# Layer 3 of a four-layer graph network: half scores spread by GpSimd, carried by one product of ones, with a chunk's stages over three turns

## The chip, the cores and the metric

The kernel runs on one core of one Trainium2 chip. The metric is the device time of one execution in microseconds (us), the median of several executions. The core has four engines that matter here, each with its own in-order queue of instructions: TensorE (PE; its weight loads are listed apart as PEld), VectorE (DVE), ScalarE (ACT) and GpSimd (POOL). A fifth, SyncE (SP), issues DMA transfers. Engines wait for each other through semaphores.

## The reference, cut to what matters

The input x has 128 graphs of 64 nodes with 256 features each, and one 64x64 adjacency serves all graphs. Four layers run one after the other, each as x = x + layer(relu(layernorm(x))). Layer 0 is a graph convolution with LSTMs over windows, layer 1 an attention over 512 edges, layer 2 a graph convolution with two batch norms. The change is in layer 3, a dense attention:

```python
def _L3_gnn_ref(h, adj_matrix, W, a):
    Wh = jnp.einsum('bnf,fo->bno', h, W)
    a1, a2 = (a[:Fout, 0], a[Fout:, 0])
    s1 = Wh @ a1
    s2 = Wh @ a2
    e = s1[:, :, None] + s2[:, None, :]
    e = jnp.where(e >= 0, e, ALPHA * e)            # ALPHA = 0.2
    e = jnp.where(adj_matrix[None] == 0, -jnp.inf, e)
    attention = jax.nn.softmax(e, axis=-1)
    return jnp.einsum('bij,bjo->bio', attention, Wh)
...
h = jnp.maximum(_layernorm(x, axis=-1), 0.0)
x = x + _L3_gnn_ref(h, adj, L3_gnn_W, L3_gnn_a)
```

The score of a pair of nodes (i, j) is the sum of two half scores, s1 of the row node i and s2 of the column node j.

## The kernel before, in words

The 8192 tokens (graph times node) are cut into 16 chunks of 512. A chunk is four tiles of 128 partitions, and a tile holds two graphs of 64 nodes. All data is fp32. Layers 0, 1 and 2 run first over all chunks and end with a batch norm over all tokens, so layer 3 can't start a chunk before layer 2 has ended. Layer 3 then takes the chunks one by one. For chunk n its stages are:

- N(n), `second_norm` (L1884 and on): TensorE transposes the output of layer 2 (8 transposes, L1893); VectorE adds it to x (L1898) and takes the statistics of the layer norm (L1902, L1903); GpSimd turns them into scale and shift (L1912 to L1915) and normalizes four tiles (L1919). `scale_o` (L1881, GpSimd) prepares the input of the transposes.
- F(n), `features`: 8 transposes of the normalized tiles (L1934), and two ScalarE copies with relu into hT (L1937).
- W(n), `project3`: for each of the four tiles two products of hT with `wext`, which holds W and one more column, W a1 (L51, through the helper `mm`); ScalarE copies the 257 columns into `wh` (L1958). Column 256 of `wh` is s1.
- S(n), `dense_scores`: four products of hT with `wa2`, which holds the column W a2 repeated 64 times (L51). Their result is s2 of every column node, laid along the free axis and repeated on 64 partitions; the two graphs of a tile go to the two halves of the partitions. VectorE adds s1 (L1970), takes the leaky relu (L1976), adds the mask (L1977) and finds the negated row maximum (L1979). ScalarE takes four exponentials with their row sums (L1982), VectorE the reciprocal of the sums (L1985).
- X(n), `turn`: TensorE transposes the four tiles of exponentials (L1993); VectorE copies one half into a block-diagonal `field`, ScalarE the other half (L1997).
- V(n), `dense_values`: four products of `field` with `wh` (L51); VectorE scales them by the reciprocals and adds them to x (L2008); SP sends the chunk to memory (L2018, L2022).

The loop `for n in range(NCH + 1)` holds, in the order of the program: N(n+2), `scale_o`(n+4), F(n+1), the first two tiles of W(n), X(n-1), the other two tiles of W(n), S(n), V(n-1). The first turn differs: it ends W(0), then does S(0) and F(1).

A recording layer may move an instruction ahead of others on its engine. An instruction that is passed to `late` (which calls `tc.keep_in_program_order`) keeps its place. In layer 3 of the kernel before, `late` is used in the first three norms and in `scale_o` only. [...] PSUM is used as four single banks (`bank`) and two pairs of banks (`pair_bank`), each taken in turn; a tile of PSUM that is taken again waits for those who read it.

Of the kernel before, what the change touches and what calls it, by code (L numbers as in the profile page):

```python
# [17 lines left out]
P = 128  # L18
# [13 lines left out]
def gnn_stack_kernel(ctx: ExitStack, tc: tile.TileContext, a: dict, out: bass.AP):  # L32
# [17 lines left out]
    def mm(o, lhsT, rhs, start=True, stop=True):  # L50
        nc.tensor.matmul(o, lhsT, rhs, start=start, stop=stop)  # L51
# [145 lines left out]

    tab2 = ctx.enter_context(tc.tile_pool(name="tab2", bufs=1))
    bdH = tab2.tile([P, P], F32, tag="bdH", name="bdH")
    wext = tab2.tile([P, 2, D + 1], F32, tag="wext", name="wext")  # L200
    wa2 = tab2.tile([P, 2, T], F32, tag="wa2", name="wa2")
    mask3 = tab2.tile([P, T], F32, tag="mask3", name="mask3")

    def late_tables():
        with ExitStack() as setup:
            s2 = setup.enter_context(tc.tile_pool(name="s2", bufs=1, side="right"))
            nc.sync.dma_start(out=wext[:, :, :D], in_=a["W3"])
            w3T = s2.tile([P, 2, D], F32, tag="w3T", name="w3T")
            nc.sync.dma_start(out=w3T, in_=a["W3T"])
            a3 = s2.tile([P, 2, 2], F32, tag="a3", name="a3")  # L210
            nc.sync.dma_start(out=a3, in_=a["a3"])

            late(nc.vector.tensor_scalar(mask3, adj2, 0.0, NEG, ALU.is_equal, ALU.mult))
            yield

            eye = s2.tile([P, T], F32, tag="eye", name="eye")
            for h in range(2):
                r = slice(h * T, (h + 1) * T)
                nc.vector.tensor_copy(eye[r, :], ident[r, r])
            an = s2.tile([P, T], F32, tag="an", name="an")  # L220
            anT = s2.tile([P, T], F32, tag="anT", name="anT")
            nc.vector.tensor_tensor(an, adj2, eye, ALU.add)
            nc.vector.tensor_tensor(anT, adjT2, eye, ALU.add)
            yield
            deg = s2.tile([P, 3], F32, tag="deg", name="deg")
            diag = s2.tile([P, T], F32, tag="diag", name="diag")
            nc.vector.tensor_tensor(diag, an, eye, ALU.mult)
            nc.vector.tensor_reduce(deg[:, 0:1], anT, AX.X, ALU.add)
            nc.vector.tensor_reduce(deg[:, 1:2], an, AX.X, ALU.add)
            nc.vector.tensor_reduce(deg[:, 2:3], diag, AX.X, ALU.add)  # L230
            yield
            dinv = s2.tile([P, 1], F32, tag="dinv", name="dinv")
            nc.vector.tensor_tensor(dinv, deg[:, 0:1], deg[:, 1:2], ALU.add)
            nc.vector.tensor_tensor(dinv, dinv, deg[:, 2:3], ALU.subtract)
            nc.gpsimd.tensor_tensor(dinv, dinv, half_power[:, 0:1], ALU.pow)
            yield
            dinv_b = s2.tile([P, P], F32, tag="dinv_b", name="dinv_b")
            nc.vector.tensor_copy(dinv_b, dinv.to_broadcast([P, P]))
            nc.vector.memset(bdH, 0.0)
            nc.vector.tensor_scalar(anT, anT, dinv, None, ALU.mult)  # L240
            yield
            p = bank()
            mm(p[:, :T], dinv_b[:T, :], ident[:T, :T])
            yield
            for h in range(2):
                r = slice(h * T, (h + 1) * T)
                nc.vector.tensor_tensor(bdH[r, r], p[r, :T], anT[r, :], ALU.mult)
            yield

            p = bank()  # L250
            for c in range(2):
                for k in range(2):
                    mm(
                        p[:, 2 * c : 2 * c + 2],
                        w3T[:, k, c * P : (c + 1) * P],
                        a3[:, k, :],
                        k == 0,
                        k == 1,
                    )
            yield  # L260
            for c in range(2):
                nc.vector.tensor_copy(wext[:, c, D:], p[:, 2 * c : 2 * c + 1])
                nc.vector.tensor_copy(wa2[:, c, :], p[:, 2 * c + 1 : 2 * c + 2].to_broadcast([P, T]))
            yield


# [1212 lines left out]
    with ExitStack() as l2:  # L1479
# [463 lines left out]
        def project3(n, tiles):  # L1943

            if n not in att3:
                wh = t4.tile([P, 4, D + 1], F32, tag="wh", name="wh", bufs=3)
                att3[n] = [wh, None, None]
            for i in tiles:
                p = bank()
                for k in range(2):  # L1950
                    mm(
                        p[:, : D + 1],
                        hT3[n][:, k, i * P : (i + 1) * P],
                        wext[:, k, :],
                        k == 0,
                        k == 1,
                    )
                nc.scalar.copy(att3[n][0][:, i, :], p[:, : D + 1])  # L1958

        def dense_scores(n):  # L1960

            wh, hT = att3[n][0], hT3.pop(n)

            p = bank()
            for k in range(2):
                hv = hT[:, k, :].rearrange("p (i o t) -> p o i t", o=2, t=T)
                for h in range(2):
                    mm(p[h * T : (h + 1) * T, : 4 * T], wa2[:, k, :], hv[:, h], k == 0, k == 1)
            e = t4.tile([P, 4, T], F32, tag="e3", name="e3")
            nc.vector.tensor_tensor(  # L1970
                e,
                p[:, : 4 * T].rearrange("p (i t) -> p i t", t=T),
                wh[:, :, D:].to_broadcast([P, 4, T]),
                ALU.add,
            )
            nc.vector.scalar_tensor_tensor(e, e, 0.2, e, ALU.mult, ALU.max)  # L1976
            nc.vector.tensor_tensor(e, e, mask3.unsqueeze(1).to_broadcast([P, 4, T]), ALU.add)  # L1977
            nmx = stat.tile([P, 4], F32, tag="nmx3", name="nmx3")
            nc.vector.tensor_reduce(nmx, e, AX.X, ALU.max, negate=True)  # L1979
            den = stat.tile([P, 4], F32, tag="den3", name="den3")  # L1980
            for i in range(4):
                nc.scalar.activation(  # L1982
                    e[:, i, :], e[:, i, :], AF.Exp, bias=nmx[:, i : i + 1], accum_out=den[:, i : i + 1]
                )
            nc.vector.reciprocal(den, den)  # L1985
            att3[n][1:] = [e, den]

        def turn(n):

            e = att3[n][1]  # L1990
            p = bank()
            for i in range(4):
                nc.tensor.transpose(p[:T, i * P : (i + 1) * P], e[:, i, :], ident)  # L1993
            f = att3[n][1] = fields[n % 2]
            for h in range(2):
                r = slice(h * T, (h + 1) * T)
                (nc.scalar.copy if h else nc.vector.tensor_copy)(  # L1997
                    f[r, :, r], p[:T, :].rearrange("p (i j) -> p i j", i=4)[:, :, r]
                )

        def dense_values(n):
            wh, f, den = att3.pop(n)
            xt = xts.pop(n)
            p = pair_bank()
            for i in range(4):
                mm(p[:, i // 2, i % 2 * D : (i % 2 + 1) * D], f[:, i, :], wh[:, i, :D])
            for i in range(4):
                nc.vector.scalar_tensor_tensor(  # L2008
                    xt[:, i, :],
                    p[:, i // 2, i % 2 * D : (i % 2 + 1) * D],  # L2010
                    den[:, i : i + 1],
                    xt[:, i, :],
                    ALU.mult,
                    ALU.add,
                )
                if n == NCH - 1 and i % 2:

                    nc.sync.dma_start(  # L2018
                        out=token_tiles(out, n)[:, i - 1 : i + 1, :], in_=xt[:, i - 1 : i + 1, :]
                    )  # L2020
            if n < NCH - 1:
                nc.sync.dma_start(out=token_tiles(out, n), in_=xt)  # L2022
# [12 lines left out]
        for _ in second:  # L2035
            pass
        scale_o(3)
        for n in range(NCH + 1):
            if 4 <= n + 4 < NCH:
                fetch(n + 4)  # L2040
            if n + 2 < NCH:
# [1 line left out]
                    pass  # L2043
            if n + 4 < NCH:
                scale_o(n + 4)
            if n == 0:
                project3(0, (2, 3))
                dense_scores(0)
                features(1)
                continue  # L2050
            if n + 1 < NCH:
                features(n + 1)
            if 0 <= n < NCH:
                project3(n, (0, 1))
            if n >= 1:
                turn(n - 1)
            if 0 <= n < NCH:
                project3(n, (2, 3))
                dense_scores(n)
            if n >= 1:  # L2060
                dense_values(n - 1)

# [1 line left out]
def _laid_out(i):  # L2064
# [65 lines left out]
```

## Time and profile before

| what | us |
|---|---|
| median of 3 runs | 2017.27 |
| lowest and highest of these | 2010.04 and 2019.0 |
| time of the profiled execution | 2013.09 |
| span of its trace | 2011.2 |
| last product of layer 2 starts | 1851.2 |
| V(0) starts, V(11) starts | 1880.45, 1975.14 |
| V(12), V(13), V(14), V(15) start | 1983.74, 1992.21, 1999.07, 2004.02 |
| between V(n) and V(n+1), n from 0 to 11 | 8.60 to 8.61 |

From 1882 to 1984 us, 102 us, TensorE is busy 102.00, VectorE 79.72, ScalarE 51.24 and GpSimd 65.66, and the granted TensorE clock is 1.00 of full speed. Over the whole span TensorE is busy 1943.8 us (97%). An fp32 product appears as two MATMUL records, a transpose as one. In a timeline a line gives the start, the length, the engine, the source line and the operation, then what it writes and reads. The chain of waits follows the work that ended last back through time.

### The profile page before, as it was taken

To read this page: it belongs to the slowest core of one execution; us is meant where nothing else is said; L and a number is where in the kernel's file an instruction comes from. 1 tells how busy PE (TensorE), PEld (TensorE's weight loads), DVE (VectorE), ACT (ScalarE), POOL (GpSimd) and SP (SyncE) were. 2 spreads that over 40 slices of the span, in tenths; PEclk is the share of its full clock that TensorE was granted. 3 is DMA by queue.
4 is the path that set the end of the run, shared out by engine and by line. 5 is a ranking of instruction groups with operands and counts; after the bars stand their busy time and mean duration, and the time that the engine had idled before them with its cause. 6 is when DMAs were issued, how large, how long until landed. Compare 5 with 4: busy or idle time off the path is not lost. (4 is left out here: it accounts for less than half of the span.)

```text
span 2011.2 us, 25608 instructions
## 1 busy us (share of the span) xinstructions
PE 1943.8 (97%) x9464; PEld 1387.3 (69%) x9464; DVE 1309.0 (65%) x2468; ACT 1141.2 (57%) x2137; POOL 428.0 (21%) x590
## 2 busy tenths in 40 slices
PE   7999999999999999999999999999998999999998
PEld 6777478866678854888666888655555775444786
DVE  8764675575475567665655655657765877886776
ACT  4353775565455547665545555566664556691544
POOL 3000031030030011310200100336554510000563
PEclk9999999999999999999999999999999999999999
DMA  8422000010010053001001000612235641022012
GB/s 291 139 78 79 0 22 1 0 43 0 1 42 1 1 190 103 22 1 43 0 0 43 1 0 31 225 65 67 107 121 190 252 153 47 0 84 84 32 64 74
DMA packets 63869, 135.60 MB, mean 67 GB/s; under 512 B 6656, under 2 KB 41344, under 8 KB 61440
## 3 DMA queue, kind: packets, MB, share of 16 engines
q1 hardware_dynamic: 57504, 109.65, 16.3%
q0 software_dynamic: 5632, 24.12, 3.2%
q8 instruction: 74, 1.21, 0.3%
q14 instruction: 51, 0.42, 0.1%
q10 hardware_dynamic: 608, 0.20, 0.1%
HBM read 87.55 MB, written 46.40 MB: 67 GB/s over the span
## 5 line engine op out<-in xcount | busy, mean ns | idle before, releaser
L746 ACT ACTIVATE gate<-gate,bias 128x256 f32<-128x256 f32 (+2 forms) x368 | 247.2, 678 | 183.0 <-DVE gate L762 100.8
L718 PE MATMUL pa<-xop,sih 128*128 128x256 f32 (+2 forms) x1056 | 342.4, 417 | 8.3 <-DVE gate L772 8.1
L718 PEld LDWEIGHTS pa<-xop,sih 128*128 128x128 f32 x1056 | 198.8, 190 | 81.5 <-issue 21.5
L718 PE MATMUL pc<-xop,wih 128*128 128x256 f32 (+2 forms) x736 | 251.1, 423 | 0.0
L762 DVE TENSOR_TENSOR gate<-pb,gate 128x256 f32<-128x256 f32 (+2 forms) x184 | 87.4, 475 | 225.6 <-PE pb L718 151.3
L718 PE MATMUL pa<-lstm_h,shh 128*128 128x256 f32 (+1 forms) x672 | 212.7, 398 | 0.0
L718 PEld LDWEIGHTS pc<-xop,wih 128*128 128x128 f32 x736 | 139.8, 190 | 51.2 <-issue 23.0
L1086 ACT ACTIVATE lr<-pair 128x1024 f32<-128x1024 f32 x128 | 124.0, 1022 | 68.6 <-PE pair L1076 60.3
L777 DVE TENSOR_TENSOR gate<-pc,gate 128x256 f32<-128x256 f32 (+2 forms) x184 | 87.5, 475 | 112.3 <-PE pc L718 112.0
L718 PEld LDWEIGHTS pa<-lstm_h,shh 128*128 128x128 f32 x672 | 127.7, 190 | 30.2
L718 PE MATMUL pc<-lstm_h,whh 128*128 128x256 f32 (+1 forms) x448 | 141.8, 398 | 0.0
L1088 DVE SCALAR_TENSOR_TENSOR lr<-lr,fold 128x1024 f32<-128x1024 f32 x64 | 83.2, 1301 | 82.0 <-ACT lr L1086 79.4
L761 ACT COPY gate<-pa 128x256 f32<-128x256 f32 (+2 forms) x184 | 75.9, 413 | 93.0 <-PE pa L718 92.6
L1045 PE MATMUL bank<-wlv,hT 128*128 128x260 f32 x480 | 121.8, 397 | 0.5 <-issue 0.5
L772 DVE TENSOR_TENSOR gate<-pa,gate 128x256 f32<-128x256 f32 (+2 forms) x184 | 87.4, 475 | 43.7 <-PE pa L718 43.1
L746 ACT ACTIVATE gate<-pa,bias 128x256 f32<-128x256 f32 (+2 forms) x184 | 93.7, 509 | 30.9 <-PE pa L718 29.4
L1045 PEld LDWEIGHTS bank<-wlv,hT 128*128 128x128 f32 x480 | 86.8, 191 | 32.2 <-issue 11.2
L766 ACT COPY gate<-pa 128x256 f32<-128x256 f32 (+2 forms) x184 | 75.1, 408 | 53.1 <-PE pa L718 52.3
L718 PE MATMUL pa<-xop,wih 128*128 128x256 f32 (+1 forms) x320 | 101.6, 399 | 2.8 <-ACT xop L699 2.7
L718 PE MATMUL pb<-xop,wih 128*128 128x256 f32 (+1 forms) x320 | 100.4, 398 | 0.0
L718 PEld LDWEIGHTS pc<-lstm_h,whh 128*128 128x128 f32 x448 | 85.1, 190 | 20.1
L500 POOL TENSOR_TENSOR shh<-whh 128x512 f32<-128x512 f32 x6 | 8.3, 1389 | 385.5 <-DMA whh<-in_WhhT 317.6
(370 smaller groups left out, 3918.6 us busy)
## 6 DMA issues: line engine op xcount, KB each, us to landing
field<-keep SPq DMA_DIRECT2D x4, 2304.0 KB
wih<-in_WihT SPq DMA_DIRECT2D x8, 1024.0 KB, 7.1
xres<-in_x SPq DMA_DIRECT2D x16, 512.0 KB, 6.2
xa<-xres POOLq DMA_DIRECT2D x16, 512.0 KB
dense<-field POOLq DMA_DIRECT2D x4, 2048.0 KB
xin<-xb SPq DMA_DIRECT2D x16, 512.0 KB, 5.2
h<-xb SPq DMA_DIRECT2D x16, 512.0 KB, 3.7
xin<-in_x SPq DMA_DIRECT2D x15, 512.0 KB, 9.9
```

What stands on the lines that cost most here:

```text
L500: keep(nc.gpsimd.tensor_tensor(o, x, y, op))
L718: ins = nc.tensor.matmul(p[:, : self.N], weights[kind, self.phase](k, q), x[k], start=first_ and kind == "ih", stop=kind == "hh" or not se ...
L746: nc.scalar.activation(out, in_, AF.Tanh if q == 2 else AF.Sigmoid, bias=bias[:, self.w - 1, 2 * q + j : 2 * q + j + 1],)
L761: nc.scalar.copy(blk[0, 0], pa[:, :N])
L762: nc.vector.tensor_tensor(blk[0, 0], pb[:, :N], blk[0, 0], ALU.add)
L766: nc.scalar.copy(blk[1, 0], pa[:, :N])
L772: nc.vector.tensor_tensor(blk[1, 1], pa[:, :N], blk[1, 1], ALU.add)
L777: nc.vector.tensor_tensor(blk[1, 0], pc[:, :N], blk[1, 0], ALU.add)
L1045: ins = nc.tensor.matmul(o, hTs[n][:, k, i * P : (i + 1) * P], wlv[:, k, cols], start=k == 0, stop=k == 1)
L1086: nc.scalar.activation(lr, p, AF.Relu)
L1088: nc.vector.scalar_tensor_tensor(lrs[1], lrs[0], fold, lrs[1], ALU.mult, ALU.add)
```

## The change

The half score s2 no longer comes from products of its own. `wext` gets one more column, W a2, so `wh` has 258 columns and column 257 of it is s2 of the node on that partition. A new stage `spread` has GpSimd multiply this column with an identity pattern `eye`: `across[p, i, t]` is s2 of node p where t is the node's number in its graph, and zero elsewhere. One product with `same_graph`, a block-diagonal matrix of ones, adds `across` over the 64 partitions of a graph, which gives s2 of column node t on all partitions of that graph. VectorE then goes on as before.

The loop has one more turn, and its order is new: N(n+2), `scale_o`(n+4), V(n-2), S(n-1), F(n+1), W(n) with all tiles, `spread`(n), X(n-1). So the stages W and `spread`, then S and X, then V of a chunk stand in three successive turns, where before they stood in two. S's product, the first transpose of X and the first product of V are passed to `late`.

```diff
-    wext = tab2.tile([P, 2, D + 1], F32, tag="wext", name="wext")
-    wa2 = tab2.tile([P, 2, T], F32, tag="wa2", name="wa2")
+    wext = tab2.tile([P, 2, D + 2], F32, tag="wext", name="wext")
+    same_graph = tab2.tile([P, P], F32, tag="same_graph", name="same_graph")
+    eye = tab2.tile([P, T], F32, tag="eye", name="eye")
...
+            nc.vector.memset(same_graph, 0.0)
             for h in range(2):
                 r = slice(h * T, (h + 1) * T)
                 nc.vector.tensor_copy(eye[r, :], ident[r, r])
+                nc.vector.memset(same_graph[r, r], 1.0)
...
             for c in range(2):
-                nc.vector.tensor_copy(wext[:, c, D:], p[:, 2 * c : 2 * c + 1])
-                nc.vector.tensor_copy(wa2[:, c, :], p[:, 2 * c + 1 : 2 * c + 2].to_broadcast([P, T]))
+                nc.vector.tensor_copy(wext[:, c, D:], p[:, 2 * c : 2 * c + 2])
...
+        def spread(n):
+
+            wh = att3[n][0]
+            hT3.pop(n)
+            across = spreads[n] = t4.tile([P, 4, T], F32, tag="across", name="across")
+            nc.gpsimd.tensor_tensor(
+                across,
+                wh[:, :, D + 1 :].to_broadcast([P, 4, T]),
+                eye.unsqueeze(1).to_broadcast([P, 4, T]),
+                ALU.mult,
+            )
 
         def dense_scores(n):
 
-            wh, hT = att3[n][0], hT3.pop(n)
-
+            wh, across = att3[n][0], spreads.pop(n)
             p = bank()
-            for k in range(2):
-                hv = hT[:, k, :].rearrange("p (i o t) -> p o i t", o=2, t=T)
-                for h in range(2):
-                    mm(p[h * T : (h + 1) * T, : 4 * T], wa2[:, k, :], hv[:, h], k == 0, k == 1)
+            late(nc.tensor.matmul(p[:, : 4 * T], same_graph, across.rearrange("p i t -> p (i t)"), start=True, stop=True))
...
-        for n in range(NCH + 1):
+        for n in range(NCH + 2):
...
-            if n == 0:
-                project3(0, (2, 3))
-                dense_scores(0)
-                features(1)
-                continue
+            if n >= 2:
+                dense_values(n - 2)
+            if 1 <= n <= NCH:
+                dense_scores(n - 1)
             if n + 1 < NCH:
                 features(n + 1)
-            if 0 <= n < NCH:
-                project3(n, (0, 1))
-            if n >= 1:
+            if n < NCH:
+                project3(n, (0, 1, 2, 3) if n else (2, 3))
+                spread(n)
+            if 1 <= n <= NCH:
                 turn(n - 1)
-            if 0 <= n < NCH:
-                project3(n, (2, 3))
-                dense_scores(n)
-            if n >= 1:
-                dense_values(n - 1)
```

More of the change, by code (lines that the diff above doesn't have):

```diff
@@ L214, in late_tables @@
             yield
-            eye = s2.tile([P, T], F32, tag="eye", name="eye")
+            nc.vector.memset(same_graph, 0.0)
             for h in range(2):
@@ L1945, in project3 @@
             if n not in att3:
-                wh = t4.tile([P, 4, D + 1], F32, tag="wh", name="wh", bufs=3)
+                wh = t4.tile([P, 4, D + 2], F32, tag="wh", name="wh", bufs=3)
                 att3[n] = [wh, None, None]
@@ L1951, in project3 @@
                     mm(
-                        p[:, : D + 1],
+                        p[:, : D + 2],
                         hT3[n][:, k, i * P : (i + 1) * P],
@@ L1957, in project3 @@
                     )
-                nc.scalar.copy(att3[n][0][:, i, :], p[:, : D + 1])
+                nc.scalar.copy(att3[n][0][:, i, :], p[:, : D + 2])
+        spreads = {}
+        def spread(n):
[8 more added lines that the diff above has]
+            )
         def dense_scores(n):
-            wh, hT = att3[n][0], hT3.pop(n)
+            wh, across = att3[n][0], spreads.pop(n)
             p = bank()
-            for k in range(2):
-                hv = hT[:, k, :].rearrange("p (i o t) -> p o i t", o=2, t=T)
-                for h in range(2):
-                    mm(p[h * T : (h + 1) * T, : 4 * T], wa2[:, k, :], hv[:, h], k == 0, k == 1)
+            late(nc.tensor.matmul(p[:, : 4 * T], same_graph, across.rearrange("p i t -> p (i t)"), start=True, stop=True))
             e = t4.tile([P, 4, T], F32, tag="e3", name="e3")
@@ L1972, in dense_scores @@
                 p[:, : 4 * T].rearrange("p (i t) -> p i t", t=T),
-                wh[:, :, D:].to_broadcast([P, 4, T]),
+                wh[:, :, D : D + 1].to_broadcast([P, 4, T]),
                 ALU.add,
@@ L1992, in turn @@
             for i in range(4):
-                nc.tensor.transpose(p[:T, i * P : (i + 1) * P], e[:, i, :], ident)
+                ins = nc.tensor.transpose(p[:T, i * P : (i + 1) * P], e[:, i, :], ident)
+                if not i:
+                    late(ins)
             f = att3[n][1] = fields[n % 2]
@@ L2005, in dense_values @@
             for i in range(4):
-                mm(p[:, i // 2, i % 2 * D : (i % 2 + 1) * D], f[:, i, :], wh[:, i, :D])
+                ins = nc.tensor.matmul(
+                    p[:, i // 2, i % 2 * D : (i % 2 + 1) * D], f[:, i, :], wh[:, i, :D], start=True, stop=True
+                )
+                if not i:
+                    late(ins)
             for i in range(4):
```

## The prediction

> **What bounds the kernel now.** I read the page's first part, then the chain of waits in layer 3 alone, since the change touches nothing else that takes time. The page says that TensorE fills the span:
>
> ```profile
> PE 1943.8 (97%) x9464; PEld 1387.3 (69%) x9464; DVE 1309.0 (65%) x2468; ACT 1141.2 (57%) x2137; POOL 428.0 (21%) x590
> ```
>
> The chain of waits over one turn of layer 3 (start, us, what) holds TensorE and nothing else:
>
> ```profile
> 1938.02 2.75 PE bank L51 x16
> 1940.78 1.93 PE pair L51 x8
> 1942.70 0.87 PE pair L1893 x8
> 1943.58 1.30 PE bank L51 x6
> 1944.88 0.87 PE pair L1934 x8
> 1945.76 0.44 PE bank L51 x2
> 1946.19 0.44 PE bank L1993 x4
> ```
>
> The turn is V 1.93, N 0.87, six and two records of W, F 0.87, X 0.44, then eight of W and the eight of S (2.75). A W record takes 1.30/6 = 0.217, so W is 16 x 0.217 = 3.48 and S is 2.75 - 1.74 = 1.01. Sum 8.60, and the V starts are 8.60 to 8.61 apart: TensorE alone sets the pace. The others wait; over the 12 turns from 1882 to 1984 us the list of waits has
>
> ```profile
> ACT e L1982 <- DVE nmx L1979: 32.8, 12, 2.9
> DVE e L1970 <- PE bank L51: 20.2, 12, 1.8
> ```
>
> VectorE idles 1.7 a turn ahead of the scores. What matters for the change is how VectorE spends the time in which ScalarE takes the exponentials. The timeline of such a turn:
>
> ```profile
> 1932.29 0.42 DVE L1970 TENSOR_TENSOR e<-bank,wh 128x256 f32<-128x256 f32 x1 [1.66 <-PE bank L51]
> 1932.74 0.42 DVE L1976 SCALAR_TENSOR_TENSOR e<-e 128x256 f32<-128x256 f32 x1
> 1933.20 0.66 DVE L1977 TENSOR_TENSOR e<-e,mask 128x256 f32<-128x256 f32 x1
> 1933.90 0.42 DVE L1979 TENSOR_REDUCE nmx<-e 128x4 f32<-128x256 f32 x1
> 1934.24 1.65 DVE L2008 SCALAR_TENSOR_TENSOR h<-pair,den,h 128x256 f32<-128x256 f32 x4
> 1934.41 0.35 ACT L1982 ACTIVATE e<-e,nmx 128x64 f32<-128x64 f32 x1 [2.85 <-DVE nmx L1979]
> 1935.88 0.18 DVE L1985 RECIPROCAL den<-den 128x4 f32<-128x4 f32 x1
> 1935.98 1.21 DVE L1898 TENSOR_TENSOR h<-pair,h 128x1024 f32<-128x1024 f32 x1
> ```
>
> The four output steps (L2008) stand between the row maximum and the reciprocal, so the 1.47 us of exponentials (1934.41 to 1935.88) pass under work. The steps between the exponentials and V, unhidden, are seen at the end of the kernel, where nothing else is left:
>
> ```profile
> 2001.64 1.29 PE L1993 MATMUL bank<-ident,e 128*64 128x128 f32 x4 [0.58 <-ACT e L1982]
> 2003.18 0.38 DVE L1997 COPY field<-bank 64x256 f32<-64x256 f32 x1
> 2003.60 0.36 ACT L1997 COPY field<-bank 64x256 f32<-64x256 f32 x1 [1.02 <-DVE field L1997]
> 2004.02 2.00 PE L51 MATMUL pair<-wh,field 128*128 128x256 f32 x8 [1.09 <-ACT field L1997]
> 2006.11 1.66 DVE L2008 SCALAR_TENSOR_TENSOR h<-pair,den,h 128x256 f32<-128x256 f32 x4 [2.54 <-PE pair L51]
> ```
>
> Three things to see: ScalarE's half of the field starts only when VectorE's has ended; V starts 0.06 after it; and the output steps start 2.09 after V's start, when all eight records are over, not after the first tile.
>
> **The change, part by part.**
>
> **Products.** S loses eight records (1.01) and gets two of 256 columns, 2 x 0.217 = 0.43. V's 1.93 is 0.19 over eight records at 0.217, and behind the 64-column weights of `wa2` I give it 0.1 back. The 258th column adds 16/257 of 0.217 = 0.01 to W. TensorE's own work per turn becomes 8.60 - 1.01 + 0.43 - 0.1 = 7.9, a gain of 0.7, if TensorE is still the bound.
>
> **GpSimd's spread.** Nearest rows: its products of 128x256 in L152 take 0.72 to 0.74, the slowest of that shape (L707) 1.59. I take 0.75 with 1.6 as the other end. GpSimd is busy 65.66/12 = 5.5 of 8.6 a turn, so it fits. It waits for the last W copy, and S follows V in the next turn, so there are 1.6 to 1.9 us to spare in the walk below: nothing on the path up to about 2.4.
>
> **The order, which is what costs.** In the built program TensorE's turn is V(n-2), S(n-1), F(n+1), W(n), then X(n-1) and N(n+3), in every other turn X first (type 1), in the others N with X's transposes between and behind it (type 2). VectorE's turn is: four output steps of V(n-2), four score steps of n-1, the reciprocal of n-1, then field and L1898 (type 1) or L1898 and field (type 2), then the statistics. So the output steps moved from behind the row maximum to ahead of the scores, and directly behind the maximum stands the reciprocal, which waits for all four exponentials. Queued behind it on VectorE are the field copy, L1898 and the statistics; TensorE waits for the field copy at V, and S stands behind V. A ring closes: V, output steps, scores, exponentials, X, field, V. Its length from the rows:
> - V's start to output steps: 2.09
> - four output steps: 1.65
> - four score steps and the start of the exponentials, 1932.29 to 1934.41: 2.12
> - first exponential (2001.14 in the same timeline) to the end of the fourth transpose (2001.64 + 1.29 = 2002.93) and 0.04: 1.83
> - field on VectorE, 2003.18 to 2003.60: 0.42; on ScalarE until V, 2003.60 to 2004.02: 0.42
>
> Sum for type 1: 8.53. In type 1 VectorE ends late: L1898 waits for N, which TensorE does after X. The fourth transpose starts 1.49 after the first exponential; 0.11 for it, 0.87 for N and 0.26 until a reader starts (F at 1936.11 is read at 1937.24: 1.13 = 0.87 + 0.26) put L1898 at 2.73; with 1.21 for it and 1.70 for the statistics (1937.22 to 1939.23 less 0.31 of field within) VectorE is free at 5.64. V began at 1.83 + 0.84 = 2.67 and its output steps could start at 4.76: late by 0.88. In type 2 L1898 starts at 1.57 (1934.41 to 1935.98) and ends at 2.78, so field comes 0.95 later than 1.83. Type 2: 8.53 + 0.88 + 0.95 = 10.36. The pair is 18.9, or 9.45 a turn against 8.60. Where the expected gain went: TensorE's 0.7 falls into its own wait for the field.
>
> **Sum.** From V(0) to V(15) there are 15 intervals. The first eleven hold an N and alternate from type 1: 6 x 8.53 + 5 x 10.36 = 103.0. The twelfth takes over the last 0.88: 9.41. Three more without N, where L1898 is gone but the ring is as long: 3 x 8.53 = 25.6. Together 138.0; before, 2004.02 - 1880.45 = 123.6. So +14.4. About half of it (35.0 against 28.9, V(11) to V(15)) is the end, where before the turns got shorter with less TensorE work (8.5, 6.9, 4.95) and a ring doesn't.
>
> The start: S(0) began at 1870.67. Now it waits for W(0)'s last copy, behind F(1), at about 1872.05, and for the spread, 0.8: 2.2 later. In exchange S(1) isn't ahead of V(0), but N(4) is. I take +2 for V(0), ends 0 and +4.
>
> **The clock of TensorE**: the row first. After layer 2, TensorE idles 4.0 us and the granted clock (last but two) is halved until about 1868, although it is mostly busy; at the end, with gaps up to 1.1, it isn't:
>
> ```profile
> 1857.00:1862.00 5.00, 4.03 (x18) 3.08 (x16) 3.94 (x15) 1.67 (x4) 2.23 (x3) 0.50 0.00 0
> 2001.00:2008.00 7.00, 3.26 (x13) 1.87 (x12) 3.75 (x11) 1.80 (x9) 0.00 (x0) 1.00 0.24 80
> ```
>
> The Trainium skill, "TensorE: Matmul & The Clock Gate", section "HAM oscillation — how this bites in real kernels", puts the point at an idle gap of some 3.4 us, and warns in the next section that small repeated idling can do it too. It speaks against this change. By the row, gaps as in the loop (in type 2 from the fourth transpose at 1.6 to V at 3.62, 2.0 at most) cost nothing; by the warning, at half clock TensorE's turn would be 2 x 7.9 = 15.8, +6.3 x 15 = +95. I go by the row. But in the last full ring TensorE has nothing between S(15) and X(15), about 4 us, so V(15) may run at half clock: eight records at 0.43 instead of 0.217, +1.7. I take +0.9, ends 0 and 1.7.
>
> **VectorE against GpSimd**: L1976 takes 0.42, L1977 0.66 in the loop and 0.43 at the end, where GpSimd is silent. "SBUF — State Buffer", section "Who interferes with whom", gives the reason: a VectorE operation with two SBUF inputs waits for a GpSimd one that reads SBUF. By that rule `across` is one more blocker, up to 0.75 a turn; by the walk it runs after the exponentials, beside L1898 and the statistics, which have one SBUF input, and costs 0. In type 2, however, the scores meet L1919 at another point, 0.64 apiece: 0 to +0.8 there, in the range (+4 in all).
>
> Everything else, the tables and a memset in the earlier layers, is under TensorE's work: 0 (uncovered, a 128x128 memset is below 0.5).
>
> Total: +2 + 14.4 + 0.9 = +17.3. On the profiled execution 2013.09 + 17.3 = 2030.4; the median is 4.2 above that execution, for reasons that the trace doesn't show: 2017.3 + 17.3 = 2034.6, rounded to 2034.
>
> **The rivals.**
> - *The ring as worked out*, 2034, own range 2027 to 2042. Against it: a wait can be a few tenths shorter than at the end, where I measured; 0.3 a turn is 4.5.
> - *More contention and slower handovers.* One output step at 2001.52 started 0.4 after V's records had ended. 0.4 to 0.7 a turn more: +6 to +10, 2042.
> - *Output steps that follow tile by tile.* If each needed only its own product, the last would end 1.24 earlier. Type 2 is held by VectorE and stays; the ten other intervals shrink: -12.4, 2022, within 0.5%. Against it: 2006.11 above.
> - *The other side: TensorE stays the bound*, because the reciprocal stalls VectorE for less than its idle time. Then 11 turns at 8.0 give -6.7, the end some -1, the start +2: 2012. It decides where the ring falls below 8.2 on average; a ring of 9.45 would have to be wrong by 1.2 in each turn. That the spread isn't hidden is no way out, it only adds.
> - *Half clock in the loop*: +45 to +95, 2060 to 2110.
>
> **How the numbers follow.** Chances: the ring 0.67, more contention 0.12, tile by tile 0.11, TensorE the bound 0.06, half clock 0.04. About 0.5%, 10 us, is what a measurement of this kernel can tell (three runs spread over 9). Faster is the fourth case less its edge, 0.05. Same holds the tile-by-tile case, the rest of the fourth and the lowest tenth of the first: 0.11 + 0.01 + 0.07 = 0.19. Slower: 0.76. The range 2021 to 2046 leaves out the fourth, the half clock and the edges of the others.
>
> **What the profile after would show.** V starts that alternate, about 8.5 and 10.4, not 8.0. VectorE idle 1.5 before the reciprocal, released by ScalarE; TensorE idle before V, released by ScalarE's field. S as two records of 0.43 together. GpSimd's spread at 0.7 to 1.6 with S waiting for it nowhere but at chunk 0. V(15) 8.5 after V(14). The prediction is wrong if TensorE stays without gaps, if output steps start before V's end, or if granted clock falls below 1.00 in the loop.

## The result, and the profile after

| | before | after |
|---|---|---|
| median (5 runs each, two more of the kernel before than above; us) | 2017.65 (2010.04 to 2019.0) | 2033.28 (2031.25 to 2037.56) |
| ratio, 95% interval | | 1.0097 (1.0078 to 1.0116) |
| span of the profiled execution | 2011.2 | 2031.5 |
| first transpose of layer 3 | 1856.23 | 1858.07 |
| V(0) starts | 1880.45 | 1884.13 |
| V(15) starts, and takes | 2004.02, 2.00 | 2022.88, 3.78 |

The kernel is slower by about 1%, and the page's first part alone wouldn't say why: every engine has nearly the busy time that it had.

```profile
PE 1948.8 (96%) x9368; PEld 1393.0 (69%) x9368; DVE 1311.1 (65%) x2469; ACT 1138.9 (56%) x2137; POOL 435.9 (21%) x606
```

The chain of waits of the changed kernel (start, us, what) no longer holds TensorE alone. This is the end of a long turn and the short turn after it (pieces called "issue", of 0.04 us and less, are left out):

```profile
1939.75 1.23 DVE h L1899
1940.98 0.33 DVE field L2010
1941.34 0.37 ACT field L2010
1941.75 1.99 PE pair L2019 x8
1943.75 0.43 PE bank L1979 x2
1944.18 0.87 PE pair L1935 x8
1945.05 3.49 PE bank L51 x16
1948.54 0.32 PE bank L2004 x2
1948.89 0.30 PE bank L2004
1949.22 0.30 PE bank L2004
1949.52 0.87 PE pair L1894 x8
1950.42 1.99 PE pair L2019 x8
```

V (L2019) at 1941.75 is reached through VectorE's sum (L1899), VectorE's half of the field and ScalarE's half (both L2010). The V starts are 10.02, 8.68, 10.02, 8.67 us apart from the second interval on: long and short turns alternate. S (L1979) is two records of 0.43 together. From the timeline of the same 19 us these lines are the ring, first the long turn (V at 1931.72), then the short one:

```profile
1931.72 1.99 PE L2019 MATMUL pair<-wh,field 128*128 128x256 f32 x8
1934.53 0.45 DVE L2025 SCALAR_TENSOR_TENSOR h<-pair,den,h 128x256 f32<-128x256 f32 x1
1936.14 0.41 DVE L1981 TENSOR_TENSOR e<-bank,wh 128x256 f32<-128x256 f32 x1
1937.04 0.42 DVE L1988 TENSOR_TENSOR e<-e,mask 128x256 f32<-128x256 f32 x1
1937.66 2.17 POOL L1920 TENSOR_SCALAR h<-h,ln_rs,ln_nm 128x256 f32<-128x256 f32 x4
1938.01 0.35 ACT L1993 ACTIVATE e<-e,nmx 128x64 f32<-128x64 f32 x1
1939.48 0.18 DVE L1996 RECIPROCAL den<-den 128x4 f32<-128x4 f32 x1 [1.56 <-ACT e L1993]
1939.75 1.23 DVE L1899 TENSOR_TENSOR h<-pair,h 128x1024 f32<-128x1024 f32 x1
1940.89 0.41 DVE L2010 COPY field<-bank 64x256 f32<-64x256 f32 x1
1941.75 1.99 PE L2019 MATMUL pair<-wh,field 128*128 128x256 f32 x8 [1.93 <-ACT field L2010]
1943.85 1.66 DVE L2025 SCALAR_TENSOR_TENSOR h<-pair,den,h 128x256 f32<-128x256 f32 x4 [0.89 <-PE pair L2019]
1945.12 2.49 POOL L1920 TENSOR_SCALAR h<-h,ln_rs,ln_nm 128x256 f32<-128x256 f32 x4
1945.43 0.41 DVE L1981 TENSOR_TENSOR e<-bank,wh 128x256 f32<-128x256 f32 x1
1945.88 0.61 DVE L1987 SCALAR_TENSOR_TENSOR e<-e 128x256 f32<-128x256 f32 x1
1946.52 0.67 DVE L1988 TENSOR_TENSOR e<-e,mask 128x256 f32<-128x256 f32 x1
1947.73 0.35 ACT L1993 ACTIVATE e<-e,nmx 128x64 f32<-128x64 f32 x1 [0.52 <-DVE nmx L1990]
1949.20 0.18 DVE L1996 RECIPROCAL den<-den 128x4 f32<-128x4 f32 x1 [1.56 <-ACT e L1993]
1949.56 0.42 DVE L2010 COPY field<-bank 64x256 f32<-64x256 f32 x1 [0.18 <-PE bank L2004]
1950.01 0.36 ACT L2010 COPY field<-bank 64x256 f32<-64x256 f32 x1 [0.32 <-DVE field L2010]
```

Read the short turn from top to bottom: V starts, 2.10 later the output steps, 1.58 later the scores, 2.30 later the first exponential, 1.83 later the field, 0.86 later V (1950.42). That is 8.67. Steps taken from start to start must add up to the interval; what makes them a ring is that each starts when the one before it lets it, as the brackets say of the output steps, the exponential and the field. The long turn is 2.81 + 1.61 + 1.87 + 2.88 + 0.86 = 10.03. In the short turn TensorE has no gap ahead of V: its four transposes X (L2004 in the chain) trickle behind the four exponentials and take 0.98 where they took 0.44 before, and N ends at 1950.39, ScalarE's half of the field at 1950.37. So there the wait for the exponentials lies inside X. In the brackets, VectorE stands idle 1.56 ahead of each reciprocal, for ScalarE, and TensorE 1.93 ahead of V. The list of waits between 1900 and 1990 us has the same two, and one that is harmless:

```profile
DVE den L1996 <- ACT e L1993: 15.6, 10, 1.6
PEld pair L2019 <- ACT field L2010: 12.1, 10, 2.2
PE pair L2019 <- ACT field L2010: 9.6, 5, 1.9
POOL across L1968 <- ACT wh L1959: 6.4, 5, 3.7
```

The last is GpSimd waiting for the last copy of W before it can start a spread. TensorE isn't listed as waiting for the spread in these turns. TensorE is busy 79.96 of these 90 us, where before it had no gap.

### The profile page after: what moved, and what is told of

It is laid out like the page before. It is cut to its first block, busy times and chain, and to the rows that moved or that the text cites. A ratio compares the mean times of both kernels' runs of the same rounds, so it can differ in the third digit from the quotient of the medians.

```text
span 2031.5 us, 25417 instructions
## 1 busy us (share of the span) xinstructions
PE 1948.8 (96%) x9368; PEld 1393.0 (69%) x9368; DVE 1311.1 (65%) x2469; ACT 1138.9 (56%) x2137; POOL 435.9 (21%) x606
## 6 DMA issues: line engine op xcount, KB each, us to landing
xin<-in_x SPq DMA_DIRECT2D x15, 512.0 KB, 10.2
```

## The experiments

The first four ran on one chip, where the kernel before took 2016.34 us; the last four on another, where it took 2008.42. The expectations are written for a kernel before of about 2017, so the ratios are what is compared. "A turn" is the mean distance of V starts in the middle of the loop.

| kernel | ratio to before (95%) | a turn, us | V(0) to V(15), us |
|---|---|---|---|
| before | 1 | 8.60 | 123.57 |
| after | 1.0097 (1.0078 to 1.0116) | 8.67 and 10.03 | 138.75 |
| output steps behind the row maximum | 1.0000 (0.9989 to 1.0011) | 8.23 | 122.52 |
| new order, old products | 1.0079 (1.006 to 1.0098) | 8.85 and 9.65 | 138.85 |
| new products, old order | 1.0315 (1.0297 to 1.0334) | irregular | |
| product of ones twice | 1.0063 (1.0045 to 1.0081) | 8.57 and 9.35 | 133.03 |
| scores ahead of V | 1.0081 (1.005 to 1.0112) | 9.75 to 10.2 | 134.67 |
| field always first | 1.0084 (1.0059 to 1.011) | 9.19 | 135.96 |
| reciprocal in the next turn | 1.0042 (1.0028 to 1.0056) | 8.55 and 8.92 | 131.37 |
| best version | 0.9987 (0.9976 to 0.9997) | 8.13 | 118.09 |

**Output steps behind the row maximum.** All stages of the change stay; only VectorE's four output steps go back to where they stood before, under the exponentials. They, the row maximum and the reciprocal are passed to `late`.

```diff
-            if n >= 2:
-                dense_values(n - 2)
+            rest = dense_values(n - 2) if n >= 2 else None   # products only
             if 1 <= n <= NCH:
-                dense_scores(n - 1)
+                dense_scores(n - 1, rest)
...
-            nc.vector.tensor_reduce(nmx, e, AX.X, ALU.max, negate=True)
+            late(nc.vector.tensor_reduce(nmx, e, AX.X, ALU.max, negate=True))
+            if between:
+                between()                                    # the four output steps
```

> Changed kernel with VectorE's order alone mended: the four output steps of a chunk stand between the row maximum and the reciprocal of the next, TensorE's order V, S, F, W, X, N is kept. Ring theory (V, output steps, scores, exponentials, X, field, V): the output steps leave the ring and cover the exponentials, the turn falls from 9.35 to 8.1 to 8.5 and VectorE's wait before the reciprocal from 1.56 to below 0.5. Eleven turns by about -1.05 and the end by about -3: 2017 to 2021 us. If the new products, the spread or TensorE's clock were the cause, VectorE's order would change little: 2030 to 2034.

Measured: 2016.07 us, ratio 1.0000. The loss is gone, all of it. The recording layer now also puts VectorE's field copy ahead of the sum in every turn; that this alone doesn't restore the time is shown by "field always first" below. The waits between 1910 and 1980 us, and the window of the same 70 us (its ends, its length, then busy time of TensorE, weight loads, VectorE, ScalarE, GpSimd, then granted clock, DMA share and GB/s):

```profile
DVE field L2012 <- PE bank L2006: 8.7, 9, 1.0
PEld pair L2021 <- ACT field L2012: 3.3, 9, 1.2
DVE den L1998 <- ACT e L1995: 0.3, 1, 0.3
```

```profile
1910.00:1980.00 70.00, 68.85 (x386) 58.26 (x385) 55.46 (x159) 34.93 (x134) 52.49 (x94) 1.00 0.20 67
```

The wait at the reciprocal fell from 15.6 in 10 turns to 0.3 once, and TensorE is busy 68.85 of 70: the bound is TensorE again, at 8.23 a turn. What this also shows is how little the new products bring: 8.60 became 8.23. The loop gained some 4 us (11 intervals at 0.37), and the total didn't, because it is lost at both ends: from the first transpose to V(0) 25.56 instead of 24.22, V(1) 9.61 after V(0), V(15) only 7.12 after V(14), where it was 4.95, and V(15) itself at half clock, 3.58 instead of 2.00.

**New order, old products.** The loop and the `late` marks of the change, but the scores as four products (eight records) with `wa2` from hT, no spread, 257 columns. The lines below are set against the changed kernel.

```diff
-            wh, across = att3[n][0], spreads.pop(n)
+            wh, hT = att3[n][0], hT3.pop(n)
...
-            late(nc.tensor.matmul(p[:, : 4 * T], same_graph, ...))
+            for k in range(2):
+                hv = hT[:, k, :].rearrange("p (i o t) -> p o i t", o=2, t=T)
+                for h in range(2):
+                    nc.tensor.matmul(p[h * T : (h + 1) * T, : 4 * T], wa2[:, k, :], hv[:, h], ...)
```

> The new order of the loop with the old scores: four products with the 64-column weights, no spread, no product of ones. Ring theory: S is not in the ring (VectorE is at the output steps while it runs), so TensorE's 0.58 us more per turn fall into its wait for the field: 2030 to 2034, turns of 8.7 and 9.6 to 10. Only the start gains, where S(0) need not wait for the spread: about -1. If the new products or the spread made the loss, the time goes back to that of the kernel before, 2018, or below.

Measured: 2031.63 us, ratio 1.0079, turns of 9.65 and 8.85, V(0) to V(15) 138.85. Without a spread and without the product of ones the loss is nearly the same, and VectorE waits for the exponentials ahead of the reciprocal as in the changed kernel (18.6 us in 9 waits, 1905 to 1980). So it is the order that costs, and not GpSimd or the new product.

**New products, old order.** The reverse: `spread(n)` just ahead of `dense_scores(n)` in the loop of before, no `late` on S, X and V.

```diff
+                spread(n)
                 dense_scores(n)
```

> The new scores (spread and one product of ones) in the old order of the loop. If TensorE is the bound, 0.67 us a turn less: 2007 to 2011. If the spread is late, S waits for it on TensorE: GpSimd does it behind the norm's four tiles and the two scale steps, and S stands in the same turn as W, so a ring VectorE statistics, GpSimd, spread, S, scores, next statistics closes at 12 to 14 us a turn: 2060 to 2085. The order of three turns would then be what makes the spread usable.

Measured: 2078.41 us, ratio 1.0315, as expected, and the worst of all. Its waits between 1910 and 1980 us, where TensorE is busy only 50.50 of 70:

```profile
DVE e L1981 <- PE bank L51: 21.0, 5, 6.1
PEld bank L51 <- POOL across L1968: 14.9, 5, 3.8
PE bank L51 <- POOL across L1968: 13.2, 5, 3.6
```

Here TensorE does wait for the spread, 13.2 in 5 waits. In this order the spread has no turn between W and S to hide in, so the change's third turn is not an ornament. What isn't needed is the place that the output steps got with it.

**Product of ones twice.** The same product a second time into the same bank (the second overwrites the first with the same numbers).

```diff
-            late(nc.tensor.matmul(p[:, : 4 * T], same_graph, ...))
+            for _ in range(2):
+                late(nc.tensor.matmul(p[:, : 4 * T], same_graph, ...))
```

> The changed kernel with the product of ones done twice over the same PSUM (0.43 us more of TensorE work in each of 16 turns). Ring theory: TensorE has slack between W and X or before V, the time stays within 1.5 us of the changed kernel, 2032 to 2035. If TensorE's work sets the pace, +7: 2040. If small idle gaps make the clock fall, the added work could win something in V(11), which ran at half clock: -1.

Measured: 2027.6 us, ratio 1.0063: more work, less time, and a miss for both theories. The extra product made the recording layer choose another order: VectorE's field copy now stands ahead of the sum in every turn, and the turns are 9.35 and 8.57 instead of 10.03 and 8.67. So the run doesn't measure what it was meant to measure, the price of 0.43 us on an idle TensorE. That more work on TensorE came out faster doesn't fit TensorE's work as what sets the pace, but with two things changed at once it is no proof. It shows that an edit of one engine's work can move another engine's queue. (The V(11) of the expectation is the one counted as V(10) here.)

**Scores ahead of V.** If S stands behind V, and V is on the ring, is it enough to let S go first?

```diff
-            if n >= 2:
-                dense_values(n - 2)
             if 1 <= n <= NCH:
                 dense_scores(n - 1)
+            if n >= 2:
+                dense_values(n - 2)
```

> Edit: in the kept order the product of ones (scores of chunk n-1) stands ahead of the attention product of chunk n-2; everything else as in the changed kernel. Ring theory: the output steps leave the ring, since the scores no longer stand behind them on TensorE; but the spread now has to be ready a whole attention product earlier, and it stands in GpSimd's queue behind the norm of a later chunk, which waits for VectorE's statistics. A second ring is worked out from the durations in the trace of the changed kernel: statistics 1.7, norm 4.3, the two scale steps 1.5, spread 0.6, product of ones 0.4, hand-overs; about 10.1 a turn, 2036 to 2042 us, with GpSimd named as what TensorE waits for ahead of the product of ones. Rival (only the output steps ahead of the scores made the changed kernel slow, the spread has room): turns of 7.9 to 8.3, 2012 to 2018 us.

Measured: ratio 1.0081. A second ring, as worked out: turns of 9.75 to 10.2, and TensorE waits for GpSimd in six of the seven turns between 1905 and 1975 us:

```profile
POOL ln_rs L1913 <- DVE ln_mv L1904: 24.1, 7, 3.7
PE bank L1979 <- POOL across L1968: 11.0, 6, 2.1
DVE den L1996 <- ACT e L1993: 10.6, 7, 2.8
```

GpSimd waits for VectorE's statistics, then has the norm and the scale steps ahead of the spread. The total is below the expected 1.009 to 1.012, though its interval reaches 1.0112. I had not counted the end, where the trace shows what S ahead of V saves: the last two intervals are 6.64 and 4.95 instead of 8.23 and 8.35.

**Field always first.** VectorE's field copy, the sum and the first of N's transposes kept in program order, so that on TensorE N stands behind X in every turn.

```diff
-            keep = late if n < 3 else lambda ins: ins
+            keep = late
...
+                if not h:
+                    late(ins)      # VectorE's half of the field
```

> Edit: the second norm's transposes and sum of a later chunk and VectorE's half of the field are kept in the order of the program, so that the field is always ahead of the sum; nothing else. Theory: the alternation goes, but not the time. In the long turns of the changed kernel the sum holds the field up by 0.95; in the short ones the sum and the statistics run late and are paid in the turn after, by 0.88. With the field always first each turn is 8.53 + 0.88 = 9.4: V starts 9.3 to 9.5 apart, total 2029 to 2034 us. Rival (the long turns alone are the fault, and the short ones show what the ring costs): every turn 8.5 to 8.7, 2022 to 2025 us.

Measured: ratio 1.0084, every turn 9.18 or 9.19 from V(3) to V(12). The alternation went and the time stayed, as expected; the 8.5 to 8.7 of the rival did not come. The turn is 0.2 shorter than I had worked out. A long and a short turn are thus one thing paid in two ways: VectorE has the sum and the statistics (1.23 and 1.7 us) to do in each turn, and whether they hold up the field or the next output steps, they lie on the ring.

**Reciprocal in the next turn.** It is needed by the output steps alone, so it can go there, and the queue behind it is free. VectorE's half of the field is kept in program order too.

```diff
-            nc.vector.reciprocal(den, den)
             att3[n][1:] = [e, den]
...
+            late(nc.vector.reciprocal(den, den))   # in dense_values, ahead of the output steps
             for i in range(4):
                 nc.vector.scalar_tensor_tensor(
```

> Edit: the reciprocal of the sums of exponentials is taken just ahead of the output steps, in the next turn, and VectorE's half of the field is kept ahead of it; output steps stay ahead of the row maximum. Ring theory: the reciprocal only blocks the queue for what stands behind it; V, output steps, scores, exponentials, transposes, field, V is as long as before. The field no longer waits behind the sum, and the reciprocal lies inside the scores: 8.9 to 9.1 a turn instead of 9.35, 2026 to 2030 us. Rival (the stall at the reciprocal is the whole loss): TensorE bound again, 8.2 a turn, 2014 to 2019 us.

Measured: ratio 1.0042, turns of 8.92 and 8.55. The loss is cut by more than half, to the lower edge of what was expected (1.0042 of 2017 is 2026; the turns are 8.74 on average, not 8.9 to 9.1), and the 8.2 of the rival did not come. In the timeline of VectorE the wait has only moved from the reciprocal to the field:

```profile
1942.27 0.42 DVE L1990 TENSOR_REDUCE nmx<-e 128x4 f32<-128x256 f32 x1
1944.97 0.42 DVE L2009 COPY field<-bank 64x256 f32<-64x256 f32 x1 [2.28 <-PE bank L2003]
```

VectorE does nothing between the row maximum and the field, because the output steps have been done. The fault is not the instruction that waits; it is that the work which used to cover the exponentials was spent ahead of them.

**A best version.** The output steps behind the row maximum, the spread ahead of `scale_o` in GpSimd's queue, and S ahead of V in the last two turns that have both.

```diff
+            if NCH - 2 < n <= NCH:
+                dense_scores(n - 1, lambda: dense_values(n - 2)())
...
                 spread(n)
+            if n + 4 < NCH:
+                scale_o(n + 4)     # was ahead of dense_values
```

> Edit: the output steps behind the row maximum as in the earlier run that restored the time, and besides: the spread ahead of the scale steps in GpSimd's queue, and in the last two turns the product of ones ahead of the attention product. Theory: in the loop TensorE is the bound at 8.1 to 8.3; at the end the last ring is shorter, since the last scores don't stand behind the attention product before (about 2 us), and the last attention product may keep the full clock because TensorE's gap before it is shorter (about 1.6 us). Total 2010 to 2014 us, faster than the kernel before by 0.1 to 0.3 %. Rival (GpSimd's queue is late at the first chunks anyway, and the end is set by the exponentials): 2015 to 2018 us, no difference.

Measured: 2004.97 us beside 2008.42 of the kernel before, ratio 0.9987 (0.9976 to 0.9997): faster by 0.13%, some 2.6 us (the medians differ by 3.5), barely clear of no difference, at the lower end of the 0.1 to 0.3% expected. V(0) to V(15) is 118.09, 5.5 less than before: 8.13 a turn in the loop, and the last intervals are 8.92, 6.64 and 4.86. The last V has the full clock (timeline):

```profile
1994.54 1.99 PE L2021 MATMUL pair<-wh,field 128*128 128x256 f32 x8 [0.91 <-ACT field L2012]
1996.63 1.66 DVE L2030 SCALAR_TENSOR_TENSOR h<-pair,den,h 128x256 f32<-128x256 f32 x4 [2.54 <-PE pair L2021]
```

The start took more than half of the gain back: from the first transpose to V(0) 27.56 us instead of 24.22. There TensorE runs out of work for 2.5 us in front of chunk 2's transposes, which wait for ScalarE's part of the norm, and then has W(1) at half clock for some time.

## Why the prediction was right

The forecast was 2034 (its sum, 2034.6, rounds to 2035), the measured median 2033.28. The mechanism, the ring and its two kinds of turn, came as forecast; that the number came within 1 us is in part luck, as the last points say. By its steps:

- **Where the gain goes.** Predicted: TensorE's saving falls into its own wait for the field. Right in the main: of the 18.70 of a long and a short turn, TensorE's own work is 2 x 8.1 (next point) and the wait ahead of the long V 1.93. The rest, some 0.54, lies between the transposes of the short turn's X.
- **Products.** S is 0.43, as worked out. V is 1.99, not 1.83: I gave back 0.1 that V's first record was thought to owe to the 64-column weights before it, and V took 0.06 more in the chain than before instead (in the timeline its records span 2.00 before and 1.99 after). With V 1.99, S 0.43, F 0.87, W 3.49, N 0.87 and X 0.44, TensorE's own turn is 8.1, not 7.9 (8.13 measured in the best version). This was hidden here, since TensorE alone isn't the bound; in a kernel where it is, I would have promised half as much again as there was (0.7 instead of 0.47). The rival "TensorE stays the bound" would have been 2012 + 11 x 0.13, or 2013.
- **Spread.** 0.62 instead of 0.75, and TensorE waits for it once, 0.82 at S(0), as predicted. The run with the old order shows what the third turn hides: it is 3% without it.
- **Ring, short turn.** Predicted 8.53, measured 8.67. The steps: 2.09 and 2.10, 1.65 and 1.58, 2.12 and 2.30, 1.83 and 1.83, 0.84 and 0.86. The one that is off is the scores (see contention).
- **Ring, long turn.** Predicted 10.36, measured 10.03. The output steps are 0.71 late (2.81 less 2.10) and not 0.88; the sum holds the field up by 1.05 (2.88 less 1.83) and not 0.95; the scores took 1.87, where I carried over 2.12.
- **Contention.** I had allowed 0 to 0.8 for VectorE against GpSimd in the long turns. It came in the short ones: beside GpSimd's L1920 (from 1945.12), L1987 takes 0.61 and L1988 0.67; in the long ones, where L1920 starts only at 1937.66, each takes 0.42. That is 0.44 in all, and the 2.12 of the forecast, taken from a turn with one slowed step, held 0.24 of it. The place was wrong: too little in the short turns, too much in the long ones.
- **Sum of the ring.** 138.0 predicted, 138.75 measured. The alternation is as counted, but errors cancel, and that is luck. Two of the short kind hold a V at half clock, V(0) and V(10), and measure 10.20 and 9.92: 3.1 more than forecast. The four other short ones add 0.6. The five long ones give back 1.7, the last four intervals (33.8 and not 35.0) another 1.2.
- **Start.** +2 predicted; first transpose to V(0) 26.06 against 24.22, +1.84.
- **Last product.** I took +0.9 between 0 and 1.7. It is the upper end: behind a gap of 3.61 us on TensorE ahead of X(15), V(15) takes 3.78 against 2.00, +1.78.
- **The clock in the loop.** I took gaps as in the loop to cost nothing. That was wrong once, at V(10), and a clock below 1.00 in the loop was among my signs that the prediction is wrong. It cost 1.25 us (9.92 for 8.67) and leaves the ring standing; the last section has the lines.
- **Total.** 1.84 + 15.18 + 1.78 = 18.8 in layer 3 of the two traced executions, against +17.3. Their spans differ by 20.3; 1.84 of the rest lies ahead of layer 3, where the edit adds only tables and executions scatter by more (layer 3's first transpose starts between 1853 and 1861 in the four kernels on the first chip), and 0.34 comes back at the end. The medians differ by 15.6. The traced execution of the kernel before (2013.09) lies 4.6 below the median of its five runs, that of the changed kernel (2033.28) is the median; this accounts for the difference. So the forecast was 1.5 short in layer 3 itself, and the 0.7 between 2034 and 2033.28 is smaller than the errors behind it.

The tile-by-tile rival fell with the timeline: in the short turn shown the output steps start 2.10 after V starts, when all eight records are over.

## What to carry to other kernels

Before moving a stage, look at what each engine does while it would otherwise wait for a round trip through another engine. Here four output steps of VectorE covered 1.5 us of exponentials, and the move took them out from under it without removing any work. Add up the ring through all engines, not the busy time of one: durations of the old trace and a queue order gave 8.53 and 10.36 us, where 8.67 and 10.03 were measured. The fix was to put 1.65 us of VectorE work back behind the row maximum while keeping the rest of the change.

## What was unexpected of the hardware

TensorE's clock fell within the loop although TensorE was 89% busy there. In the changed kernel five gaps of 1.93 us stand between 1900 and 1980 us, one ahead of each long V. Four had no effect. After the fifth (1977.22 to 1979.15) V(10) took 3.67 us instead of 1.99. The windows of 5 us around it, with the granted clock last but two:

```profile
1970.00:1975.00 5.00, 5.00 (x29) 4.42 (x28) 4.86 (x17) 1.73 (x4) 2.15 (x4) 1.00 0.09 29
1975.00:1980.00 5.00, 3.07 (x19) 2.55 (x18) 3.35 (x10) 2.39 (x11) 4.25 (x7) 0.93 0.23 76
1980.00:1985.00 5.00, 5.00 (x22) 4.17 (x21) 2.40 (x9) 0.77 (x2) 3.87 (x8) 0.73 0.00 2
1985.00:1990.00 5.00, 4.97 (x29) 4.06 (x28) 2.73 (x6) 3.28 (x14) 0.62 (x1) 1.00 0.33 108
```

The Trainium skill, "TensorE: Matmul & The Clock Gate", section "HAM oscillation — how this bites in real kernels", speaks of idle gaps beyond some 3.4 us; this one was 1.93, and the measurement decides. In the other runs, with gaps of 2.18 and 2.06 us (scores ahead of V) V ran slow twice more (3.32 and 2.77 us), while one more gap of 2.06 cost nothing. In the seven other kernels with a V(0) to V(15) in the table, where no gap between V(1) and V(14) is over 0.96 us, V ran slow there never. But short gaps are not safe as such: at the start of the changed kernel's layer 3 two gaps of 0.81 and 0.97 us, with X between them, were followed by V(0) at half clock, 3.47 us. What decides between a gap that costs and one that doesn't is not settled by these runs. The price at V(10) was 1.25 of the 1.68 us that it took longer: the interval after it was 9.92 where the short turn is 8.67.
